# The inverse transform over w from quarters of the width, with row sums and last butterflies on GpSimd

## The chip, the cores and the metric

The kernel runs on one core of a Trainium2 chip. The metric is the device time of one execution in microseconds; a figure for a kernel is the median of several runs. The profile comes from one further execution that was recorded by the hardware profiler. Engine names are those of the profile: PE is TensorE (PEld its weight loads), DVE is VectorE, ACT is ScalarE, POOL is GpSimd, and SP is the engine whose queue issues the DMAs.

## The reference

The input x has the shape (4, 256, 256, 64), float32: batch, height h, width w, channels. Two layers follow one another. The change lies in layer 0.

```python
h  = pw(ln(x, g1, b1), w_te, b_te)                   # 64 -> 128 channels
F  = fft2(h, axes=(1, 2))
fc = gelu(pw(concat([real(F), imag(F)]), w_fc, b_fc))  # 256 -> 256
re, im = fc[..., :HID], fc[..., HID:]
sp = real(ifft2(re + 1j * im, axes=(1, 2)))
x1 = x + pw(sp, w_tp, b_tp)                          # 128 -> 64
h2 = pw(ln(x1, g2, b2), w_fe, b_fe)                  # 64 -> 128
d  = gelu(depthwise3x3(h2, w_dw) + b_dw)
x  = x1 + pw(d, w_fp, b_fp)                          # 128 -> 64
```

Layer 1 takes a moving average over h as the trend, passes the remainder through a spectral filter of 128 modes per channel, and adds both. The kernel applies it as one 256x256 matrix per channel.

## The kernel before

**Transforms.** All Fourier transforms are products with tables of cosines and sines. The forward transform over h runs in chunks of columns of x (`forward_h`): layer norm, sums and differences of mirrored columns (`halves`, L371 and L387), sums and differences of the upper and lower half of the height (`halves_h`, L394), products with the table dh (`transform`, L408), and a store to the DRAM buffer y_d. Only frequencies 0 to 128 of h are kept, since the input is real.

**Spectral stage.** The h-frequencies of an image come in groups of four (128 is carried with frequency 0), and a group is worked on in two "prs" of two frequencies each (the first group of an image has three). For one pr, `transform_w` (L502) transforms over w, `mix` multiplies by the channel matrix (ps_p, L527) with a copy to g (L539), `both` forms the product's values for +w and −w (L548), `activate` is the gelu on ACT (L552), `fold` takes a sum and a difference on GpSimd (L559), `project` multiplies by w_tp (ps_z, L584), and `turn` transposes to w-frequencies on the partitions (L597) and copies to zt (L599). When both prs of a group are in zt, `back_w` transforms back over w:

```python
for r, tbs in enumerate(((ci, nsi), (si, ci))):
    for ri, tb in enumerate(tbs):
        nc.tensor.matmul(ps[:, r * KG * C : (r + 1) * KG * C],
            tb[:, t, :], zt[:, t, ri].rearrange("p k c -> p (k c)"), ...)
```

t is the parity of the w-frequency. A group takes eight matmuls with 128 output partitions (columns 0 to 127 of w) and 256 moving columns (L618); the even part is copied (L628), and the odd part is subtracted and added (L629, L630), which gives columns 128 to 255 and 0 to 127. Two DMAs (L632) store the group in u_d.

**Convolution stage.** A chunk is eight columns of w. `load_u` (L666) loads their spectrum from u_d, `back_h` (L684) transforms back over h, `residual` (L695, L699) adds x, `measure`, `norm` and `scaled` are the layer norm (L313 to L316 on DVE, the power L322 and the scaling L327 on GpSimd), `to_channels` transposes (L722, L729), `row_sums` forms four sums and differences of neighbouring rows on DVE (L738, L742, L743), and `first`, `products`, `rest` are the matmuls of the 3x3 kernel over rows (L760, L775); gelu, projection and store follow (L826, L832, L852, L867).

**Order of work.** The order on PE, DVE, ACT and POOL is that in which the program issues (`manual_schedule`); SP's queue takes the DMAs in the order of their calls. Before the spectral stage, `starting(n)` runs 35 times (S0), with a forward chunk and two blocks of layer 1's matrices each. Then `period(n)` runs: a forward chunk at most, one group of the spectral stage (prs i and i+1, with i = 2(n − S0)), and one convolution chunk at most, each in a fixed interleaving that the call list in `period` (L1067 to L1134) writes out. Chunks of different age are in different steps: j[0] is loaded and measured, j[1] becomes row sums, j[2] and j[3] are in the products, j[4] is stored. `chunk_at` says which chunk enters in which period: the first chunk of image b may enter when the last group of that image has been stored (`opened`), at n = S0 + 35, 67, 100 and 132, and each image has 32 chunks. So there are periods of the spectral stage with the forward transform (n = 35 to 69), of all three stages (to 127), of spectral stage and convolution (to about 166), and of convolution alone, followed by layer 1.

Of the kernel before, what the change touches and what calls it, by code (L numbers as in the profile page):

```python
# [12 lines left out]
F32 = mybir.dt.float32  # L13
# [24 lines left out]
def _tables():  # L38
# [44 lines left out]
    for par in range(2):  # L83
# [6 lines left out]
    back = lambda m: np.concatenate([m[0::2, :P], m[1::2, :P]], axis=1)  # L90
# [7 lines left out]
        "ci": back(cos),  # L98
        "si": back(sin),
        "nsi": back(-sin),  # L100
# [22 lines left out]
def conv_seq_kernel(ctx: ExitStack, tc: tile.TileContext, a: dict, tables: bass.AP, out: bass.AP):  # L123
# [36 lines left out]
    ci, si, nsi = halves("ci"), halves("si"), halves("nsi")  # L160
# [171 lines left out]
    def forward_h(pool):  # L332
# [57 lines left out]
        def halves_h(j):  # L390
            xt = chunks.pop(j)
            for i, op in enumerate((ALU.add, ALU.subtract)):
                x0, x1 = (xt[:, t].rearrange("p f w c -> p (f w c)") for t in range(2))
                nc.vector.tensor_tensor(sums[j][:, i], x0, x1, op)  # L394

        def transform(j):
# [5 lines left out]
            yt = pool.tile([P, 2, 2, WH, 2, C], F32, tag="yt", name=f"yt_{j}")  # L402
# [42 lines left out]
    def spectral(pool):  # L445
# [17 lines left out]
        def begin(j):  # L463
            yb = groups[j]
            blocks = [(yb, k) for k in range(KG)]
            if j % NG == 0:

                yr = pool.tile([P, 2, 2, 2 * C], F32, tag="yr", name=f"yr_{j}", bufs=1)
                for r in range(2):
                    for part, mask in enumerate((plain, turned)):  # L470
                        at = ((r + part) % 2) * C
                        nc.vector.tensor_tensor(
                            yr[:, :, r, part * C : (part + 1) * C],
                            yb[:, :, 0, at : at + C],
                            mask.unsqueeze(2).to_broadcast([P, 2, C]),
                            ALU.mult,
                        )
                blocks = [(yr, 0), (yr, 1)] + blocks[1:]
            zt = pool.tile([P, 2, 2, KG, C], F32, tag="zt", name=f"zt_{j}")
            groups[j] = zt  # L480
            per_group[j] = [blocks[i : i + 2] for i in range(0, len(blocks), 2)]
# [109 lines left out]
        def turn(pr):  # L591

            zt, zs = groups[pr["g"]], pr["zs"]
            nf = zs.shape[1]
            ps = bank(f"ps_zt_{pr['n']}")
            for i in range(nf // P):
                nc.tensor.transpose(ps[:, i * P : (i + 1) * P], zs[:, i * P : (i + 1) * P], ident)  # L597
            nb = nf // N
            nc.scalar.copy(  # L599
                zt.rearrange("p t r k c -> p k (t r) c")[:, pr["slot"] : pr["slot"] + nb],  # L600
                ps[:, :nf].rearrange("p (j q c) -> p j q c", j=nb, c=C),
            )

        def back_w(pr):
            if not pr["last"]:
                return
            b, g = divmod(pr["g"], NG)
            if g == 0:
                u_ds[b] = spill.tile([P, N, 2, C], F32, tag="u_d", name=f"u_d_{b}")
            zt = groups.pop(pr["g"])  # L610
            ut = pool.tile([P, 2, KG, 2, C], F32, tag="ut", name=f"ut_{pr['g']}")

            pss = []
            for t in range(2):
                ps = bank(f"ps_u_{pr['g']}_{t}")
                for r, tbs in enumerate(((ci, nsi), (si, ci))):
                    for ri, tb in enumerate(tbs):
                        nc.tensor.matmul(  # L618
                            ps[:, r * KG * C : (r + 1) * KG * C],
                            tb[:, t, :],  # L620
                            zt[:, t, ri].rearrange("p k c -> p (k c)"),
                            start=ri == 0,
                            stop=ri == 1,
                        )
                pss.append(ps)
            even, odd = (ps.rearrange("p (r k c) -> p r k c", r=2, c=C) for ps in pss)
            u0, u1 = (ut[:, wt].rearrange("p k r c -> p r k c") for wt in range(2))
            nc.scalar.copy(u0, even)  # L628
            nc.vector.tensor_tensor(u1, u0, odd, ALU.subtract)  # L629
            nc.vector.tensor_tensor(u0, u0, odd, ALU.add)  # L630
            for wt in range(2):
                nc.sync.dma_start(  # L632
                    u_ds[b][g * KG : (g + 1) * KG, wt * P : (wt + 1) * P].rearrange(
                        "k p r c -> p k (r c)"
                    ),
                    ut[:, wt].rearrange("p k r c -> p k (r c)"),
                )

        def of(f):
# [13 lines left out]
            back_w=of(back_w),  # L653
        )

    def convolution(pool):
# [3 lines left out]
        TD, XN, FS = 4, 1, 2  # L660
# [4 lines left out]

        def load_u(j):  # L666
            b, q = j
            ucs[j] = pool.tile([P, W, 2, C], F32, tag="uc", name=f"uc_{name(j)}")
            nc.sync.dma_start(ucs[j], u_ds[b][:, q * W : (q + 1) * W])
# [8 lines left out]
        def back_h(j):  # L678

            uc = ucs.pop(j)  # L680
            pss = [bank(f"ps_s_{name(j)}_{i}") for i in range(2)]
            for r, tb in enumerate((ihr, ihi)):
                for i in range(2):
# [3 lines left out]
                        uc[i * C : (i + 1) * C, :, r, :],  # L687
# [45 lines left out]
        def row_sums(j):  # L733

            td = pool.tile([P, 4, NP, P], F32, tag="td", name=f"td_{name(j)}", bufs=TD)
            by_row = lambda lo: tt[:, :, lo : lo + N].rearrange("p j (i r) -> p r j i", r=2)
            for r, k in ((0, 0), (1, 3)):
                nc.vector.tensor_tensor(  # L738
                    td[:, k], by_row(0)[:, r], by_row(2)[:, r], ALU.subtract
                )  # L740
            even, odd = by_row(1)[:, 0], by_row(1)[:, 1]
            nc.vector.tensor_tensor(td[:, 1], odd, even, ALU.add)  # L742
            nc.vector.tensor_tensor(td[:, 2], odd, even, ALU.subtract)  # L743
            ts[j] = td
# [9 lines left out]
        def products(j, ks):  # L754
# [4 lines left out]
            for (k, par), ps in pss.items():  # L759
# [3 lines left out]
                    ts[j][:, k].rearrange("p j i -> p (j i)"),  # L763
# [7 lines left out]
            for k in ks:  # L771
                for g in by_turns:
# [5 lines left out]
                        td[lo : lo + C, k, at : at + n, :].rearrange("p j i -> p (j i)"),  # L778
# [100 lines left out]
        def of(f):  # L879
# [4 lines left out]
            load_x=of(load_x),  # L884
            back_h=of(back_h),
# [143 lines left out]
    def opened(b):  # L1029

        return divmod(KH * (b + 1) + 2, 2)

    chunk_at, at = {}, 0
    for b in range(B):
        at = max(at, S0 + sum(opened(b)) + 1)
# [31 lines left out]
    def period(n, f, s, c):  # L1067
# [4 lines left out]

        alone = not any(j)
        early = alone or s.done(i - 3)
# [10 lines left out]
        if alone and not s.done(i - 3):  # L1085
# [10 lines left out]
        c.row_sums(j[1])  # L1096
        s.turn(i - 2)
        s.back_w(i - 3)
        c.scaled(j[0])
        c.rest(j[3])  # L1100
        if early:
            if not alone:
                f0.square(n)
            f0.measure(n)
            f0.norm(n)
        s.mix(i)
        c.combine_rest(j[3])
        s.both(i)
        s.project(i - 1)
        s.x(i + 1)  # L1110
        if not alone or s.done(i - 3):
# [9 lines left out]
        if not early:  # L1121
            f0.square(n)
            f0.measure(n)
            f0.norm(n)
        s.turn(i - 1)
        s.back_w(i - 2)
# [9 lines left out]
    with in_order, ExitStack() as right:  # L1136
        with (
# [14 lines left out]
            for n in range(S0, S0 + opened(B - 1)[0] + 1):  # L1152
                period(n, f, s, c)
        with tc.tile_pool(name="seq", bufs=1, side="left", reuse_waits="tile") as seq:
            mts = [matrix_load(seq, c) for c in range(0, CG, CM)]
            xc = x2_load(seq, 0, 0, 1)
            for n in range(S0 + opened(B - 1)[0] + 1, END):
# [49 lines left out]
```

## Time and profile before

Three runs took 4693.13 to 4697.26 us, median 4695.19. The profiled execution took 4693.89 itself; its span is 4692.1.

| | value |
|---|---|
| median of the runs | 4695.19 us |
| profiled execution, own time | 4693.89 us |
| its span | 4692.1 us |
| granted TensorE clock | 0.99 |
| DMA | 653.31 MB, 139 GB/s on average |
| L618, return over w | 2048 records, 468.8 us |
| L738, L742, L743, row sums | 128 x 4 instructions of 128x512, 167.2 + 86.9 + 86.9 us |
| L394, halves over h | 256 of 128x512, 220.3 us |
| L559, fold on GpSimd | 520, mean 1280 ns |

How to read it: a float32 matmul leaves two records. The page gives the busy share of each engine over the whole span, and in 40 slices of about 117 us; what binds has to be read for each stage. A group of instructions is named by line, engine, operation and tiles, with its busy time, the mean of one, and the idle time of the engine ahead of it, with what ended that idle time. An arrow "<-" in brackets names the instruction whose end released it.

### The profile page before, as it was taken

What the parts mean: (1) busy time and instruction counts of PE and PEld (TensorE: products, weight loads), DVE (VectorE), ACT (ScalarE), POOL (GpSimd) and SP (SyncE); (2) the same over time, 40 slices, a digit from 0 to 9 for tenths busy, and PEclk for the clock granted to TensorE, in tenths of its full rate; (3) what the DMA queues carried; (4) which work ended last, traced back from release to release, by engine and by line L of the source; (5) the groups of instructions that cost most, each with busy time, mean ns of one, the idle gap of its engine ahead of it and who ended that gap; (6) DMA issues with size and microseconds to landing.
All of it is one profiled execution on the core that took longest, in us unless ns stands there. A gap on an engine that the chain in (4) does not pass through costs nothing.

```text
span 4692.1 us, 65967 instructions
## 1 busy us (share of the span) xinstructions
PE 4595.7 (98%) x23371; PEld 2601.2 (55%) x23371; DVE 3800.2 (81%) x6051; ACT 2511.1 (54%) x3686; POOL 1945.5 (41%) x1038
## 2 busy tenths in 40 slices
PE   8989999899999999999999999999999999999999
PEld 4545555555555555555555556556555455554444
DVE  7998888999999999999999877777777899982222
ACT  2337877666666666666666656655565333331111
POOL 4556666655555554445555334333333333320000
PEclk9999999999999999999999999999999999999999
DMA  5664444434334333333443332332332422319998
GB/s 178 199 192 144 143 133 138 126 116 125 125 125 124 125 123 125 122 121 120 124 124 119 104 100 85 107 96 90 95 96 76 157 99 98 100 59 311 324 324 277
DMA packets 759726, 653.31 MB, mean 139 GB/s; under 512 B 39693, under 2 KB 644319, under 8 KB 759272
## 3 DMA queue, kind: packets, MB, share of 16 engines
q1 hardware_dynamic: 759400, 649.11, 44.5%
q8 instruction: 187, 3.06, 0.3%
q14 instruction: 139, 1.14, 0.1%
HBM read 363.76 MB, written 285.21 MB: 138 GB/s over the span
## 4 chain that ended last, share of the span: by engine, by line
PE 87%; DVE 2%; DMA 2%; SPq 1%; ACT 0%; issue 0%; POOL 0%; DVEq 0%; POOLq 0%; ACTq 0%
PE ps_h_c L760 18%; PE ps_h_c L775 10%; PE ps_u L618 9%; PE ps_p L527 9%; PE ps_o L997 8%; PE ps_z L584 6%; PE ps_x L502 5%; PE ps_f_c L832 5%; PE ps_s_c L684 5%; PE ps_y L408 3%; PE ps_t_c L722 3%; PE ps_ft_c L852 3%; PE ps_zt L597 3%; DMA xc<-x_d 1%; DVE g L548 0%; SPq L977 0%
## 5 line engine op out<-in xcount | busy, mean ns | idle before, releaser
L559 POOL TENSOR_TENSOR g<-g 128x512 f32<-128x512 f32 (+1 forms) x520 | 660.5, 1280 | 1100.2 <-ACT g L552 996.4
L760 PE MATMUL ps_h_c<-td_c,wc_main 128*128 128x512 f32 x2048 | 921.3, 592 | 0.0
L548 DVE TENSOR_TENSOR g<-ps_p,g 128x512 f32<-128x512 f32 x1040 | 688.5, 683 | 86.6 <-ACT g L539 68.6
L552 ACT ACTIVATE g<-g,b_fc 128x1024 f32<-128x1024 f32 (+1 forms) x520 | 582.0, 1146 | 187.7 <-DVE g L548 187.6
L322 POOL TENSOR_TENSOR rstd_c<-var_c,minus_half 128x16 f32<-128x16 f32 x128 | 419.8, 3279 | 594.6 <-DVE var_c L316 594.6
L539 ACT COPY g<-ps_p 128x512 f32<-128x512 f32 (+1 forms) x520 | 302.8, 584 | 665.7 <-PE ps_p L527 660.0
L322 POOL TENSOR_TENSOR rstd<-var,minus_half 128x16 f32<-128x16 f32 x128 | 382.8, 2990 | 526.4 <-DVE var L316 403.1
L760 PEld LDWEIGHTS ps_h_c<-td_c,wc_main 128*128 128x128 f32 x2048 | 376.3, 190 | 373.7 <-issue 305.1
L775 PEld LDWEIGHTS ps_h_c<-td_c,wc_half 64*128 64x128 f32 x4032 | 416.7, 187 | 238.5 <-issue 194.1
L775 PE MATMUL ps_h_c<-td_c,wc_half 64*128 64x128 f32 (+1 forms) x4032 | 513.3, 392 | 0.0
L527 PE MATMUL ps_p<-xs,wp 64*128 64x512 f32 (+1 forms) x2080 | 498.4, 594 | 1.1 <-ACT xs L511 1.0
L618 PE MATMUL ps_u<-zt,tab 128*128 128x256 f32 x2048 | 468.8, 382 | 0.0
L997 PE MATMUL ps_o<-xc,mt 128*128 128x512 f32 x1024 | 445.0, 596 | 16.8 <-DMA xc<-x_d 16.8
L618 PEld LDWEIGHTS ps_u<-zt,tab 128*128 128x128 f32 x2048 | 383.2, 192 | 48.1 <-DVE g L548 0.3
L826 ACT ACTIVATE h_c<-h_c,b_conv 128x1024 f32<-128x1024 f32 x256 | 280.5, 1146 | 224.2 <-DVE h_c L821 224.1
L1011 DVE TENSOR_SCALAR oc<-ps_o,b_fp 128x512 f32<-128x512 f32 x128 | 96.2, 751 | 363.4 <-PE ps_o L997 342.6
L811 DVE TENSOR_TENSOR h_c<-h_c,ps_h_c 128x512 f32<-128x512 f32 x512 | 316.9, 680 | 69.7 <-PE ps_h_c L775 66.8
L800 DVE TENSOR_TENSOR h_c<-h_c,ps_h_c 128x512 f32<-128x512 f32 x256 | 175.7, 687 | 233.5 <-PE ps_h_c L775 225.0
L502 PEld LDWEIGHTS ps_x<-tab,yb 128*64 128x64 f32 x4064 | 279.1, 137 | 116.5 <-issue 88.8
L997 PEld LDWEIGHTS ps_o<-xc,mt 128*128 128x128 f32 x1024 | 195.0, 191 | 266.0 <-issue 235.3
L584 PE MATMUL ps_z<-g,w_tp 128*64 128x512 f32 x1024 | 333.7, 614 | 6.5 <-POOL g L559 3.9
L502 PE MATMUL ps_x<-tab,yb 128*64 128x128 f32 x4064 | 319.0, 274 | 0.2 <-PE ps_z L584 0.2
(125 smaller groups left out, 7205.0 us busy)
## 6 DMA issues: line engine op xcount, KB each, us to landing
y_d<-yt SPq DMA_DIRECT2D x256, 256.0 KB, 2.5
yb<-y_d SPq DMA_DIRECT2D x256, 256.0 KB, 3.1
x_c<-in_x_dram SPq DMA_DIRECT2D x128, 512.0 KB, 4.2
u_d<-ut SPq DMA_DIRECT2D x256, 256.0 KB, 2.5
uc_c<-u_d SPq DMA_DIRECT2D x128, 512.0 KB, 3.4
x_d<-st SPq DMA_DIRECT2D x128, 512.0 KB, 3.9
xc<-x_d SPq DMA_DIRECT2D x64, 1024.0 KB, 7.9
out_dram<-oc SPq DMA_DIRECT2D x256, 256.0 KB, 4.1
```

What stands on the lines that cost most here:

```text
L322: nc.gpsimd.tensor_tensor(rstd, var, minus_half.to_broadcast([P, n]), ALU.pow)
L502: nc.tensor.matmul(ps[r * C : (r + 1) * C, j * N + t * P : j * N + (t + 1) * P], blk[:, t, k, r * C : (r + 1) * C], tb[:, t, :], start=Tru ...
L527: nc.tensor.matmul(ps[:, :nf], wp[rows, cols], rhs[rows], start=True, stop=r == 1 or not pr["special"],)
L548: nc.vector.tensor_tensor(gt[:, i, :nf], re, gt[:, 1, :nf], op)
L552: nc.scalar.activation(g, g, AF.Gelu, bias=b_fc[:, half : half + 1])
L559: nc.gpsimd.tensor_tensor(g[:, 0], g[:, 0], g[:, 1], op)
L584: nc.tensor.matmul(ps[r * C : (r + 1) * C, :nf], w_tp, d[:, :nf], start=True, stop=True)
L618: nc.tensor.matmul(ps[:, r * KG * C : (r + 1) * KG * C], tb[:, t, :], zt[:, t, ri].rearrange("p k c -> p (k c)"), start=ri == 0, stop=ri == 1,
L760: nc.tensor.matmul(ps, wc_main[:, par, k, :], ts[j][:, k].rearrange("p j i -> p (j i)"), start=True, stop=False,)
L775: nc.tensor.matmul(pss[k, par][:, s * P : (s + n) * P], wc_half[lo : lo + C, k, :], td[lo : lo + C, k, at : at + n, :].rearrange("p j i -> ...
L811: nc.vector.tensor_tensor(g, g, m, (ALU.add, ALU.subtract)[r])
L997: nc.tensor.matmul(ps[:, :nf], mts[i // CM][:, i % CM, t, to * P : (to + 1) * P], xc[:, t, :, :, i, :], start=t == 0, stop=t == 1,)
```

## The change

The return over w is computed from quarters of the width. For frequencies of one parity, the tables bc (cosines) and bs (sines) cover the columns 0 to 63 only, with 64 output partitions: two groups j and j+1 are worked on together and lie in the two halves of the 128 output partitions, with real and imaginary parts side by side in 512 moving columns. A period takes four such matmuls (`back_w(n)`: parity 0 of a pair of groups in one period, parity 1 in the next). The sines are copied by ACT, and `combine_w` forms the cosine part minus and plus the sine part with real and imaginary parts swapped. `finish_w` forms the sum of both parities into `odd` and, one period later, the difference into `even` (2·even − sum), one 128x1024 instruction each on DVE, and spills each to its own buffer, u0_d and u1_d, again two DMAs in a period. Of the 256 columns, the quarters are columns 0 to 63, 65 to 128, 129 to 191 and so on, two of them in mirrored order, and `load_u` and `back_h` read those reversed, with real and imaginary parts swapped. The first columns of the other three quarters are computed apart, once for each image (`other_columns`), and column 0 gets one more addition (`first_column`); chunks at the quarters' ends are loaded in two DMAs.

Besides, `halves_h` and `row_sums` are issued on GpSimd instead of DVE. The buffers change: yt 1, zt 4 (allocated in `turn`), us 1, ut0 2, ut1 1, td in two tiles with 3 each. In `period`, the forward chunk's statistics are always taken in the middle, `back_w`, `combine_w` and `finish_w` are called once each, and `transform` is called early where there is no convolution and late where there is. Images open at n = S0 + 36, 69, 101 and 134, and the schedule is two periods longer.

```diff
-    back = lambda m: np.concatenate([m[0::2, :P], m[1::2, :P]], axis=1)
+    bc = np.zeros((P, 2, P // 2))
+    bs = np.zeros((P, 2, P // 2))
+    for par in range(2):
+        bc[:, par] = cos[par::2, : P // 2]
+        bs[:, par] = sin[par::2, : P // 2]
+        bs[:, par, 0] = 0.25 * (cos, sin)[par][par::2, P // 2]
+    bc[:, :, 0] *= 0.5
...
         def halves_h(j):
...
-                nc.vector.tensor_tensor(sums[j][:, i], x0, x1, op)
+                nc.gpsimd.tensor_tensor(sums[j][:, i], x0, x1, op)
...
+        steps, ended = {}, {}
+        for j in range(0, B * NG, 2):
+            at = (max(i for i, pr in enumerate(prs) if pr["g"] == j + 1) + 3) // 2
+            steps[at], steps[at + 1], ended[at + 2] = (j, 0), (j, 1), j
...
+        def back_w(n):
+            if n not in steps:
                 return
...
+            j, par = steps[n]
+            pss = [bank(f"ps_u_{j}_{par}_{i}") for i in range(2)]
+            for ps, tb in zip(pss, (bc, bs)):
+                for h in range(2):
+                    nc.tensor.matmul(
+                        ps[h * C : (h + 1) * C],
+                        tb[:, par, :],
+                        groups[j + h][:, par].rearrange("p r k c -> p (r k c)"),
+                        start=True,
+                        stop=True,
+                    )
+            if par:
+                del groups[j], groups[j + 1]
+            us = pool.tile([P, 2, KG, C], F32, tag="us", name=f"us_{j}_{par}", bufs=1)
+            nc.scalar.copy(us.rearrange("p r k c -> p (r k c)"), pss[1])
+            parts[n] = pss[0].rearrange("p (r k c) -> p r k c", r=2, c=C), us
...
+        def combine_w(n):
...
+            nc.vector.tensor_tensor(dst[:, 0], cs, us[:, ::-1], ALU.subtract)
+            nc.vector.tensor_tensor(dst[:, 1], cs[:, ::-1], us, ALU.add)
+            half_sums.setdefault(j, []).append(ut)
...
+        def finish_w(n):
+
+            flat = lambda t: t.rearrange("p k q r c -> p (k q r c)")
+            if n in ended:
+                j = ended[n]
+                even, sums = half_sums.pop(j)
+                nc.vector.scalar_tensor_tensor(
+                    flat(even), flat(even), 2.0, flat(sums), ALU.mult, ALU.subtract
+                )
+                spill_w(j, 1, even)
+            if n in steps and steps[n][1]:
...
+                nc.vector.tensor_tensor(flat(odd), flat(even), flat(odd), ALU.add)
+                spill_w(j, 0, odd)
...
+            for h in range(2):
+                k = (g + h) * KG
                 nc.sync.dma_start(
+                    u_ds[b][i][k : k + KG].rearrange("k q s r c -> s (k q) (r c)"),
+                    ut[h * C : (h + 1) * C].rearrange("p k q r c -> p (k q) (r c)"),
                 )
...
+        quarters = ((0, 0, False), (1, 1, True), (1, 0, False), (0, 1, True))
...
+        def first_column(j):
+            if j[1] == 0:
+                col = ucs[j][:, 0]
+                nc.vector.tensor_tensor(col, col, firsts.pop(j)[:, ::-1], ALU.add)
...
+        def other_columns(j):
...
+            for i in range(2):
+                nc.sync.dma_start(v[:, 2 * i : 2 * i + 2], u_ds[b][i][:, :, 0])
...
+            nc.sync.dma_start(fixed[b], v[:, 3:6])
...
-                        uc[i * C : (i + 1) * C, :, r, :],
+                        uc[i * C : (i + 1) * C, ::-1, 1 - r, :]
+                        if down
+                        else uc[i * C : (i + 1) * C, :, r, :],
...
         def row_sums(j):
...
+            nc.gpsimd.tensor_tensor(ts[j][1], odd, even, ALU.add)
+            nc.gpsimd.tensor_tensor(ts[j][2], odd, even, ALU.subtract)
             for r, k in ((0, 0), (1, 3)):
-                nc.vector.tensor_tensor(
-                    td[:, k], by_row(0)[:, r], by_row(2)[:, r], ALU.subtract
+                nc.gpsimd.tensor_tensor(
+                    ts[j][k], by_row(0)[:, r], by_row(2)[:, r], ALU.subtract
                 )
-            even, odd = by_row(1)[:, 0], by_row(1)[:, 1]
-            nc.vector.tensor_tensor(td[:, 1], odd, even, ALU.add)
-            nc.vector.tensor_tensor(td[:, 2], odd, even, ALU.subtract)
...
         c.scaled(j[0])
         c.rest(j[3])
-        if early:
-            if not alone:
-                f0.square(n)
-            f0.measure(n)
-            f0.norm(n)
+        c.row_sums(j[1])
+        if not alone:
+            f0.square(n)
+        f0.measure(n)
+        f0.norm(n)
         s.mix(i)
         c.combine_rest(j[3])
+        s.back_w(n - S0)
         s.both(i)
+        s.combine_w(n - S0)
         s.project(i - 1)
         s.x(i + 1)
-        if not alone or s.done(i - 3):
+        if not alone:
             f2.transform(n - 2)
         fn.load(n + 1)
         c.activate(j[3])
...
+        c.other_columns(j[0])
         s.turn(i - 1)
-        s.back_w(i - 2)
+        s.finish_w(n - S0)
         s.activate(i, 0)
         s.activate(i, 1)
         s.fold(i)
```

## The prediction

> **What bounds the kernel now.** I read the busy totals and slices of the page first, then its chain and its costliest groups, then the stretches of each stage, and last the timeline of one period of each stage.
>
> ```profile
> PE 4595.7 (98%) x23371; PEld 2601.2 (55%) x23371; DVE 3800.2 (81%) x6051; ACT 2511.1 (54%) x3686; POOL 1945.5 (41%) x1038
> ...
> PE   8989999899999999999999999999999999999999
> ...
> DVE  7998888999999999999999877777777899982222
> ...
> POOL 4556666655555554445555334333333333320000
> ...
> L559 POOL TENSOR_TENSOR g<-g 128x512 f32<-128x512 f32 (+1 forms) x520 | 660.5, 1280 | 1100.2 <-ACT g L552 996.4
> L618 PE MATMUL ps_u<-zt,tab 128*128 128x256 f32 x2048 | 468.8, 382 | 0.0
> ```
> TensorE is at 98%, and the return over w (L618) is 469 us of it. VectorE stands at 90% and more in the middle; GpSimd looks free at 41%. That last figure is an average, so I go by stage (stretch, length, busy time of PE, PEld, DVE, ACT, POOL, clock, DMA share, GB/s):
>
> ```profile
> 60.00:330.00 270.00, 264.73 (x929) 156.49 (x927) 266.96 (x354) 97.17 (x145) 154.40 (x60) 1.00 0.63 197
> 390.00:850.00 460.00, 460.00 (x2638) 266.08 (x2637) 396.06 (x605) 366.47 (x542) 293.73 (x181) 1.00 0.47 138
> 960.00:2590.00 1630.00, 1626.47 (x9199) 952.76 (x9196) 1533.91 (x2482) 1011.60 (x1484) 819.92 (x438) 1.00 0.40 123
> 2640.00:3640.00 1000.00, 999.25 (x5704) 594.59 (x5702) 761.43 (x1258) 585.02 (x863) 365.79 (x215) 1.00 0.30 93
> 3690.00:4180.00 490.00, 490.00 (x2383) 266.40 (x2382) 450.19 (x747) 189.70 (x268) 155.25 (x60) 1.00 0.28 94
> ```
> Starting (matrices beside the forward transform) is VectorE's: 267 of 270. The other four are TensorE's: the spectral stage alone (about 35 periods of 15.34 us), all three stages (57 of 29.65), spectral with convolution (37), convolution only (33 of 16.4). In the second stretch GpSimd is busy 64%, the most of the four, and there its work stands in a loop:
>
> ```profile
> 516.00 2.54 POOL L559 TENSOR_TENSOR g<-g 128x512 f32<-128x512 f32 x2 [3.21 <-PE ps_u L618]
> 519.08 0.59 PE L584 MATMUL ps_z<-g,w_tp 128*64 128x512 f32 x1
> 520.38 1.88 PE L408 MATMUL ps_y<-xb,tab 128*64 128x512 f32 x7
> 522.78 1.99 PE L527 MATMUL ps_p<-xs,wp 64*128 64x512 f32 x8
> 524.93 2.74 DVE L548 TENSOR_TENSOR g<-ps_p,g 128x512 f32<-128x512 f32 x4 [1.60 <-ACT g L539]
> 527.58 1.28 DVE L371 TENSOR_TENSOR xb<-xt 128x512 f32<-128x512 f32 x2
> 527.71 3.62 PE L618 MATMUL ps_u<-zt,tab 128*128 128x256 f32 x16
> 528.90 1.29 DVE L387 TENSOR_TENSOR xt<-xb 128x512 f32<-128x512 f32 x2
> 530.23 1.29 DVE L394 TENSOR_TENSOR xb<-xt 128x512 f32<-128x512 f32 x2
> ```
> Columns: start, duration, engine, line, operation, out<-in, count. A fold ends at 518.54; its projection, the next product ps_p and the products of L548 follow, done by 527.58, 9.04 us later. The last lines (halves over w, halves over h) hang on that end only by VectorE's order; nobody on GpSimd waits for them.
>
> **What the Trainium skill says.** TensorEngine Tiling (Array Packing), Theoretical Speedup: an output side of at most 64 allows up to twice the rate. The trace agrees: four 64-wide matmuls of 512 columns (L408; a matmul leaves two records) take 1.81 us start to start in a period of all three stages, eight 128-wide ones of 256 columns (L618), as many columns in all, 3.46. GPSIMD Engine Reference, 3.1: a GpSimd tensor_tensor add is priced 1.96 times VectorE's; here 1280 ns (L559) against 693 (L738), 1.85 times. The same page, section 7, puts a higher price on reads that step over 8 bytes; the new row sums step exactly 8, and no row shows that. SBUF — State Buffer, Who interferes with whom: a VectorE instruction with two SBUF inputs and a GpSimd instruction that reads SBUF exclude each other. The trace agrees, and both sides pay:
>
> ```profile
> 905.87 3.11 POOL L559 TENSOR_TENSOR g<-g 128x512 f32<-128x512 f32 x2
> 907.89 3.95 DVE L387 TENSOR_TENSOR xt<-xb 128x512 f32<-128x512 f32 x2
> 916.20 1.08 PE L597 MATMUL ps_zt<-ident,zs 128*128 128x128 f32 x4 [4.20 <-ACT zs L588]
> 917.07 4.92 PE L618 MATMUL ps_u<-zt,tab 128*128 128x256 f32 x16
> ```
> Undisturbed those pairs take 2.54 and 1.29. The last two lines are what an idle of 4.20 us does to TensorE: 1.08 for 0.66 and 4.92 for 3.62, together 1.7 us more.
>
> **The change, part by part.**
>
> *Return over w on TensorE.* Per period eight 128x256-column matmuls become four of 64-wide form: 3.46 goes, 1.81 comes, −1.65 us. Over 130 periods that is 214 us if TensorE is what ends the period.
>
> *VectorE per period of all three stages.* Row sums leave: 2×0.69 + 2×0.68 = 2.74 (in the trace with GpSimd's waits near 2.4 net). Halves over h leave: 2×0.65, 1.3. The two combines replace L629 and L630 one for one. One finishing operation on 128x1024 with two SBUF inputs comes: 1.21 by the row of L695. From 28.4 to about 25.9.
>
> *GpSimd per period of all three.* From 15.2 us: 4×1.28 of row sums and 2×1.28 of halves, 7.7, to 22.9. Their collisions with VectorE's two-input operations cost each side about 2 us.
>
> *Starting, 35 periods of 9.16.* VectorE-bound; L394 there takes 2.82 for two behind GpSimd, and leaves. But GpSimd must now deliver before L408, and TensorE has 264.73 of 270. I take −8; 0 to −20.
>
> *Spectral alone, the step that decides.* GpSimd's order in a period becomes: power, halves over h of the chunk before (2), fold of one group (2), scaling, fold of the other (2). The fold now queues behind halves over h, which wait for the halves over w on VectorE, which queue behind the combine, which queues behind the products of L548. And those hang on the previous period's fold, by the chain read above. So a loop closes: fold end to products' end 9.04; combine 1.41; halves over w 2.61; halves over h 2×1.28 = 2.56; fold 2.54; handoffs 0.1: 18.26 us, against 15.34 now. Nothing in it overlaps. Onto it: the finishing operation stands on VectorE directly behind the halves over w and waits for nothing, so it takes the shared read first: +1.15, 19.4. TensorE's own work in the period is about 13.5, so it idles over 4 us in one piece, ahead of the projection that the loop goes through; by the two lines above that is a slower clock, +1.7 (bounds 0 and, if all TensorE pieces of the loop run cold, 2.9): 21.1. Over 34 periods: (21.1 − 15.34)×34 = +195. Bounds: the bare loop +100, with the lock +138, everything cold +235.
>
> *All three, 57 periods.* TensorE 29.65 − 1.65 = 28.0; VectorE 25.9 and about 2 of port waits, 28. GpSimd's queue (power 3.3, scaling 2.0, row sums 5.1, power 2.95, halves, fold) now ends shortly before the fold's projection is due. So not all of 1.65 is realised: −1.2 each, −68; bounds −20 and −94.
>
> *Spectral with convolution, 37 periods.* VectorE is at 76%, GpSimd at 37%, no halves there: −1.65 each, −61.
>
> *Convolution only, 33 periods.* Row sums queue on GpSimd behind power and scaling of the next chunk. In the trace scaling ends at 3967.26, row sums end 5.12 later at 3972.4, and the row products of 16.37 later have little left: +0.45 each, +15; bounds 0 and +60.
>
> *Seams, four images.* A new chunk's columns now come from a finished pair: finishing operation at the period's end, spill 2.5, load 3.4 by the page's DMA table, and the return over h stands first on TensorE in the next period: 5 to 6 us each where there was half a period or more of slack. On top come nine small operations and the small loads and a store of the other three columns on SP's queue, and two periods more in the schedule (168 to 170). +25; bounds 10 and 50.
>
> *Layer 1.* Untouched: 0. The split loads at quarter ends stay under a period of slack: 0.
>
> Sum: −8 + 195 − 68 − 61 + 15 + 25 = +98. The profiled execution took 4693.89 itself (span 4692.1), so 4791.9; the median of the runs shown, 4695.19, is 1.3 above that execution, well inside every bound. I take **4792**.
>
> **Rivals.**
> - *The fold does not close a loop* (faster). If the engines' slack lets halves over h run early enough, spectral alone stays at 15.34 or falls by 1.65: 4597 down to 4541, about 4570. For it: TensorE holds the chain at 87% and only that was cut. Against it: GpSimd's order, where the fold cannot pass halves over h.
> - *Row sums are dear on GpSimd.* At 8-byte steps 1.9 us each instead of 1.28, +2.5 a period: all three loses 0.5 where it should gain 1.2 (+97), convolution only +13: 4902. For it: no GpSimd row with such a step. Against: the skill's threshold lies above 8 bytes.
> - *The bare loop.* Lock and clock cost nothing: spectral alone +100, sum +3, about 4697. For it: GpSimd may get its read first, and the idle may split in two. Against: the lines at 905 and 916.
>
> **How the numbers follow.** The forecast (4720 to 4880) gets 0.62, no loop 0.14, dear row sums 0.14, the bare loop 0.10. The range 4690 to 4900 holds the first, half of the third and half of the fourth, near 0.8. A difference below 0.2% (9 us) cannot be told from none. Faster: no loop 0.14 and a fifth of the bare loop, 0.16; same 0.04; slower 0.80.
>
> **What would show it.** Spectral alone near 21 us a period, TensorE idle about 6 of them in front of ps_z with GpSimd's fold as releaser, and slower matmuls after; all three near 28.4; spectral with convolution shorter by 1.6; row sums near 1.28 each. It is wrong if the period of spectral alone is below 17, if the folds do not wait for halves over h, or if a seam costs more than 15 us.

## The result, and the profile after

The changed kernel took 4723.49 us in the median of four runs (4718.87 to 4729.3), the kernel before 4694.16 beside it (4691.67 to 4697.26): a ratio of 1.0063 with a 95% interval of 1.0045 to 1.008. That is 29 us slower, where the prediction had 97 and a range of 4690 to 4900. The sign was right, and so was the mechanism in the stage that decides it, the spectral stage alone; the size was more than three times too large, above all through the term for all three stages. The profiled execution took 4729.3 us itself, with a span of 4727.5.

The page of the changed kernel, the lines that answer to those shown of before:

```profile
PE 4438.6 (94%) x22347; PEld 2295.4 (49%) x22347; DVE 3607.9 (76%) x5451; ACT 2529.2 (53%) x3686; POOL 2796.4 (59%) x1806
...
PE   8987777778999999999999999999999899999999
...
DVE  7886667678999999999999877777778688871222
...
POOL 5876666668887878688878655555555455530000
PEclk9998888889999999999999999999999999999999
...
L565 POOL TENSOR_TENSOR g<-g 128x512 f32<-128x512 f32 (+1 forms) x520 | 703.9, 1364 | 632.0 <-ACT g L558 632.0
```

The fourth to ninth slices are new: TensorE is at 70 to 79% there, its clock at 0.8. The stretches say the same (stretch, length, PE, PEld, DVE, ACT, POOL, clock, DMA share, GB/s):

```profile
390.00:850.00 460.00, 342.55 (x1792) 165.47 (x1792) 313.37 (x425) 278.57 (x405) 292.30 (x182) 0.83 0.37 101
2130.00:2330.00 200.00, 200.00 (x1153) 105.08 (x1149) 190.72 (x290) 134.88 (x197) 159.34 (x101) 1.00 0.45 135
2900.00:3400.00 500.00, 500.00 (x2917) 269.90 (x2915) 387.25 (x619) 314.91 (x462) 264.76 (x192) 1.00 0.35 102
```

In the first of them, the spectral stage alone, no engine is full, which is what a loop of waits between engines looks like. In the other two TensorE is full as it was before.

The starts of the groups ps_y, ps_u and ps_o in the two traces give the time by stage:

| from, to | before | after | difference | forecast |
|---|---|---|---|---|
| start to the 33rd ps_y (starting) | 340.5 | 334.8 | −5.7 | −8 |
| to the 68th ps_y (spectral alone) | 533.3 | 696.5 | +163.2 | +195 |
| to the last ps_y (all three) | 1763.7 | 1653.5 | −110.2 | −68 |
| to the last ps_u (spectral, convolution) | 995.5 | 968.3 | −27.2 | −61 |
| to the first ps_o (convolution only) | 593.0 | 598.4 | +5.4 | +15 |
| layer 1 | 466.1 | 476.1 | +10.0 | 0 |
| seams, lying in the rows above | | | | +25 |
| sum | 4692.1 | 4727.5 | +35.4 | +98 |

Layer 1's 10 us are no part of the change: with the same code, the profiled executions of this study have 464 to 478 us there, and one kernel that was profiled twice had 476 and 473. Steady periods went from 15.34 to 20.48 us (spectral alone), from 29.47 and later 29.81 to 27.73 (all three), from 27.75 to 26.01 (spectral with convolution), and stayed at 16.37 (convolution only).

One thing shifts between two rows: images open later now, so two chunks of the convolution move from the row of all three stages to the next one. By the starts of ps_s_c the two rows hold 60 and 36 chunks before, 58 and 38 after. A chunk is worth some 14 us there (an estimate: 29.47 − 15.34).

The timeline of one period of the spectral stage alone, changed kernel (start, duration, engine, line, operation, count, and in brackets the idle time before and its releaser):

```profile
513.95 2.50 POOL L565 TENSOR_TENSOR g<-g 128x512 f32<-128x512 f32 x2
515.27 2.34 PE L590 MATMUL ps_z<-g,w_tp 128*64 128x512 f32 x3 [5.13 <-POOL g L565]
...
519.97 1.89 PE L416 MATMUL ps_y<-xb,tab 128*64 128x512 f32 x7
...
522.38 1.99 PE L533 MATMUL ps_p<-xs,wp 64*128 64x512 f32 x8
...
524.52 2.74 DVE L554 TENSOR_TENSOR g<-ps_p,g 128x512 f32<-128x512 f32 x4 [6.19 <-ACT g L545]
...
527.18 0.68 DVE L652 TENSOR_TENSOR ut<-ps_u,us 128x512 f32<-128x512 f32 x1
...
528.37 1.28 DVE L379 TENSOR_TENSOR xb<-xt 128x512 f32<-128x512 f32 x2
...
529.69 1.29 DVE L395 TENSOR_TENSOR xt<-xb 128x512 f32<-128x512 f32 x2
530.90 1.22 DVE L671 SCALAR_TENSOR_TENSOR ut<-ut,ut 128x1024 f32<-128x1024 f32 x1
531.15 3.33 POOL L402 TENSOR_TENSOR xb<-xt 128x512 f32<-128x512 f32 x2 [3.42 <-DVE xt L395]
...
534.45 2.48 POOL L565 TENSOR_TENSOR g<-g 128x512 f32<-128x512 f32 x2
535.76 2.34 PE L590 MATMUL ps_z<-g,w_tp 128*64 128x512 f32 x3 [5.13 <-POOL g L565]
```

This is the predicted loop, link by link: fold, ps_z, ps_p, the products of L554, combine (L652), halves over w, halves over h on GpSimd (3.33 for two, with the finishing operation L671 just ahead of it on VectorE), the next fold. TensorE idles 5.13 us ahead of ps_z, and the three ps_z then take 2.34.

### The profile page after: what moved, and what is told of

Read it like the earlier page. It is cut to its first block, busy times and chain, and to the rows that moved or that the text cites. A ratio compares the mean times of both kernels' runs of the same rounds, so it can differ in the third digit from the quotient of the medians.

```text
span 4727.5 us, 63507 instructions
## 1 busy us (share of the span) xinstructions
PE 4438.6 (94%) x22347; PEld 2295.4 (49%) x22347; DVE 3607.9 (76%) x5451; ACT 2529.2 (53%) x3686; POOL 2796.4 (59%) x1806
## 4 chain that ended last, share of the span: by engine, by line
PE 81%; DVE 6%; POOL 5%; issue 4%; DMA 2%; ACT 2%; SPq 1%; POOLq 0%; DVEq 0%; ACTq 0%
PE ps_h_c L865 18%; PE ps_h_c L880 10%; PE ps_o L1104 8%; PE ps_p L533 7%; PE ps_z L590 5%; PE ps_x L508 5%; PE ps_f_c L937 5%; PE ps_y L416 5%; PE ps_s_c L784 4%; PE ps_u L629 4%; PE ps_t_c L824 3%; PE ps_ft_c L957 3%; POOL xb L402 2%; PE ps_zt L607 2%; DVE g L554 1%
## 5 line engine op out<-in xcount | busy, mean ns | idle before, releaser
L565 POOL TENSOR_TENSOR g<-g 128x512 f32<-128x512 f32 (+1 forms) x520 | 703.9, 1364 | 632.0 <-ACT g L558 632.0
L554 DVE TENSOR_TENSOR g<-ps_p,g 128x512 f32<-128x512 f32 x1040 | 687.5, 682 | 233.3 <-ACT g L545 215.3
L330 POOL TENSOR_TENSOR rstd_c<-var_c,minus_half 128x16 f32<-128x16 f32 x128 | 371.8, 2905 | 478.5 <-DVE var_c L324 468.8
L590 PE MATMUL ps_z<-g,w_tp 128*64 128x512 f32 x1024 | 354.2, 670 | 195.9 <-POOL g L565 192.5
L402 POOL TENSOR_TENSOR xb<-xt 128x512 f32<-128x512 f32 x256 | 350.9, 1390 | 220.5 <-DVE xt L395 215.1
L1104 PE MATMUL ps_o<-xc,mt 128*128 128x512 f32 x1024 | 450.9, 603 | 20.3 <-DMA xc<-x_d 20.3
L330 POOL TENSOR_TENSOR rstd<-var,minus_half 128x16 f32<-128x16 f32 x128 | 372.8, 2913 | 64.1 <-DMA xt<-in_x_dram 34.6
L508 PEld LDWEIGHTS ps_x<-tab,yb 128*64 128x64 f32 x4064 | 297.3, 149 | 149.4 <-issue 129.4
L508 PE MATMUL ps_x<-tab,yb 128*64 128x128 f32 x4064 | 345.3, 295 | 0.0
L1116 ACT ACTIVATE oc<-ps_o,b_fp 128x512 f32<-128x512 f32 x128 | 87.9, 687 | 384.5 <-PE ps_o L1104 307.5
```

The lines of the kernel that those rows point to most:

```text
L330: nc.gpsimd.tensor_tensor(rstd, var, minus_half.to_broadcast([P, n]), ALU.pow)
L402: nc.gpsimd.tensor_tensor(sums[j][:, i], x0, x1, op)
L508: nc.tensor.matmul(ps[r * C : (r + 1) * C, j * N + t * P : j * N + (t + 1) * P], blk[:, t, k, r * C : (r + 1) * C], tb[:, t, :], start=Tru ...
L554: nc.vector.tensor_tensor(gt[:, i, :nf], re, gt[:, 1, :nf], op)
L565: nc.gpsimd.tensor_tensor(g[:, 0], g[:, 0], g[:, 1], op)
L590: nc.tensor.matmul(ps[r * C : (r + 1) * C, :nf], w_tp, d[:, :nf], start=True, stop=True)
```

## The experiments

All start from the changed kernel. Times are medians, or a single run where no interval stands. The period is that of the spectral stage alone unless said otherwise, as a mean over 24 steady periods, taken from the starts of ps_y. In some runs single periods alternate between two or more lengths; where the recorded expectations name such a period (19.45 for the first run), it is the median.

### Halves over h: which engine, and where in the order

First, back on VectorE:

```diff
-                nc.gpsimd.tensor_tensor(sums[j][:, i], x0, x1, op)
+                nc.vector.tensor_tensor(sums[j][:, i], x0, x1, op)
```

> The changed kernel with one part undone: halves over h are issued on VectorE again. Loop theory (the fold queues behind halves over h on GpSimd, which hang on the previous fold): the loop opens, a period of the spectral stage alone falls from 20.5 us to about 14.4 (TensorE 13.7, VectorE with 1.3 more near 14.4), the whole to about 4723 - 33 x 6 + 10 = 4535 us. Rival A (GpSimd is simply too slow for its 12 us of work with the collisions): the period falls by what leaves GpSimd, 2.6 to 3.4, to about 17.5, the whole to about 4625. Rival B (TensorE's low clock holds the period up by itself): the period stays over 19.

Measured: 4690.09 us, 0.9996 of before (0.9987 to 1.0005). The period is 19.3 (single ones 18.2 to 20.4), not 14.4. Of the three expectations only the last gives the right number, and for another reason: TensorE's clock is 0.97 in the stage, and most of the stage's chain lies on VectorE. The timeline:

```profile
714.53 1.28 DVE L379 TENSOR_TENSOR xb<-xt 128x512 f32<-128x512 f32 x2
...
715.85 2.36 DVE L395 TENSOR_TENSOR xt<-xb 128x512 f32<-128x512 f32 x2
716.21 3.13 POOL L565 TENSOR_TENSOR g<-g 128x512 f32<-128x512 f32 x2 [2.31 <-ACT g L558]
...
718.25 3.95 DVE L402 TENSOR_TENSOR xb<-xt 128x512 f32<-128x512 f32 x2
719.31 2.34 POOL L335 TENSOR_TENSOR xt<-xt,rstd 128x1024 f32<-128x1024 f32 x1
```

Each pair on VectorE takes 1.29 when it is alone. Here halves over w run into the fold and halves over h into fold and scaling, 2.36 and 3.95: 3.7 us of waiting, and the finishing operation (in one period of this trace 2.92 us for 1.21) still stands ahead of the next products. The same stretch of the kernel before:

```profile
528.90 1.29 DVE L387 TENSOR_TENSOR xt<-xb 128x512 f32<-128x512 f32 x2
529.63 0.59 ACT L628 COPY ut<-ps_u 128x512 f32<-128x512 f32 x1 [1.14 <-PE ps_u L618]
530.12 2.19 ACT L552 ACTIVATE g<-g,b_fc 128x1024 f32<-128x1024 f32 x2
530.23 1.29 DVE L394 TENSOR_TENSOR xb<-xt 128x512 f32<-128x512 f32 x2
531.35 2.55 POOL L559 TENSOR_TENSOR g<-g 128x512 f32<-128x512 f32 x2 [3.20 <-PE ps_u L618]
```

There the gelu (L552) stood on ACT behind the copy of ps_u, so the fold began 3.77 us after the products' end at 527.58, when VectorE's two-input operations were all but done. The new return over w comes earlier, and the combine stands ahead of the halves: the fold and the halves now meet. That this order is why they meet is read from the two timelines; no run puts the old order back by itself. The period is long with halves over h on either engine; only the chain differs.

Second, on GpSimd, but behind the fold:

```diff
-        f1.halves_h(n - 1)
+        if not alone:
+            f1.halves_h(n - 1)
...
         s.fold(i)
+        if alone:
+            f1.halves_h(n - 1)
```

> Halves over h stay on GpSimd, but in the spectral stage alone they are issued behind the fold that they preceded. GpSimd has the same work in another order. Loop theory: the fold no longer waits for VectorE's halves over w, the period falls from 20.5 to about 13.8 (TensorE's own work), the whole to about 4723 - 33 x 6.7 = 4502 us. Rival A (too much work on GpSimd): the period stays at 20.5, the whole near 4720. Rival B (clock): over 19.

Measured: 4609.77 us, 0.9818 (0.9803 to 0.9832), most periods 16.91, the mean 17.0. GpSimd has the same work, so the order is shown to be worth about 3.5 us a period, and rivals A and B fall. Part of the 3.5 comes with the shorter idle of TensorE: its clock is 0.99 in this run's stage, where the changed kernel has 0.83. But 13.8 was not reached. The chain of this run goes over the fold (4.01 us for two, beside the finishing operation's 2.29), halves over h, and ps_y, which now waits for them.

### The finishing operation and the clock, each by itself

```diff
+        if alone:
+            s.finish_w(n - 1 - S0)
         s.mix(i)
...
-        s.finish_w(n - S0)
+        if any(chunk_at.get(n + 1 - k) for k in range(5)):
+            s.finish_w(n - S0)
```

> In the spectral stage alone the finishing operation on VectorE (128x1024, two SBUF inputs) moves from right behind the halves over w to the middle of the next period, where VectorE idles 6 us. The loop itself stays. Port theory (it takes the shared read just before halves over h, which then take 3.33 us for two instead of 2.55): the period falls by 0.8 to 1.2 us, from 20.5 to about 19.5, the whole by about 30 us. Without that price: no change.

Measured: 4702.85 us, period 19.76 (single ones 19.2 to 20.3), which is 0.7 less. Halves over h return from 3.33 to 2.50 for two. The price is real and a little over half of the 1.15 in the forecast.

```diff
         s.mix(i + 1)
+        if alone:
+            ps = bank(f"warm_{n}")
+            for _ in range(4):
+                nc.tensor.matmul(ps, ident, tab[:, :512], start=True, stop=True)
```

> In each period of the spectral stage alone four matmuls of 128x512 are added, written to a bank that nobody reads, where TensorE idles 5.1 us before ps_z. Clock theory (the idle costs about 1.1 us of slower matmuls in the loop): the matmuls after the wait return to 1.1 us for three ps_z and 0.6 for nine ps_x, the period falls from 20.5 to about 19.4 although TensorE has 3.4 us more to do, the granted clock in the stage rises from 0.83 to 1.00. If the clock costs nothing in the loop: 20.5 stays. The output is the same.

Measured: 4661.23 us, period 18.79, clock 1.00 in the stage. The timeline from the added matmuls on:

```profile
539.26 3.70 PE L1238 MATMUL warm<-tab,ident 128*128 128x512 f32 x8
...
544.47 1.86 PE L590 MATMUL ps_z<-g,w_tp 128*64 128x512 f32 x3 [1.50 <-POOL g L565]
...
546.60 0.71 PE L508 MATMUL ps_x<-tab,yb 128*64 128x128 f32 x9
```

3.70 us of work that nobody needs make every period 1.69 shorter. The three ps_z take 1.86 rather than 2.34, and part of that is now a wait for the fold's second half; nine ps_x take 0.71, where the run without these matmuls needed 2.07 for eleven. The gain is more than the 1.1 expected here. It equals the 1.7 of the prediction, but that figure was read from other matmuls (ps_zt and ps_u, behind an idle of 4.20 us), so that it fits this closely is partly luck.

### The change without its moves to GpSimd

Halves over h and row sums back on VectorE (nc.gpsimd replaced by nc.vector in `halves_h` and `row_sums`).

> The changed kernel with both moves to GpSimd undone: row sums and halves over h on VectorE, the new return over w and its new order stay. Row-sum theory (VectorE is next in the stage of all three, and moving the row sums is what lets TensorE's gain show): VectorE has 26.5 + 1.3 + 2.7 us, above TensorE's 27.7, so a period of all three rises from the 27.83 of the run with halves over h on VectorE to 29.5 to 30, the whole from 4690 to about 4790 us. Rival (TensorE stays the bound there in any case): 27.8 and about 4690. In the spectral stage alone both expect 19.4, as in that run, since there are no row sums in it. The power in the convolution should take 3.28 us again if it is the row sums on VectorE that lengthen it, 2.90 if not.

Measured: 4925.79 us, 1.0498 (1.0481 to 1.0516). The period of the spectral stage alone is 19.4, as expected. Those of all three alternate between 30.5 and 34.4, 32.4 in the mean, well over the 29.5 to 30 expected; the rival, 27.8, falls. A stretch of a little over four periods:

```profile
1406.00:1543.30 137.30, 123.97 (x678) 65.08 (x677) 132.64 (x195) 80.14 (x118) 67.67 (x35) 0.98 0.38 114
```

VectorE is busy 97%, TensorE 90%. Against the run with only halves over h on VectorE (27.83), the row sums' move is worth 4.6 us a period, more than the 2.7 us of their own length. How much of that is VectorE's load and how much its fixed order with the statistics in mid-period was not separated. The mean of the power (L330, convolution) in this run, and in the run with the row sums on GpSimd, from the groups of each:

```profile
L330 POOL TENSOR_TENSOR rstd_c<-var_c,minus_half 128x16 f32<-128x16 f32 x128 | 421.1, 3290 | 614.3 <-DVE var_c L324 573.2 <-PE ps_h_c L880 41.2
```

```profile
L330 POOL TENSOR_TENSOR rstd_c<-var_c,minus_half 128x16 f32<-128x16 f32 x128 | 371.8, 2905 | 480.8 <-DVE var_c L324 444.1 <-PE ps_h_c L880 36.7
```

The row sums on VectorE are what lengthened the power to 3.29. Undone in this sequence, the change's parts are worth: the new return over w in its new order about +235 us (by the same rows as in the table +119 in the spectral stage alone and +139 in all three), the row sums' move on top of it −236, the move of halves over h on top of both +33. In another sequence the shares could differ.

### Towards a faster version

Late halves over h and the finishing operation elsewhere, the two diffs above together:

> Halves over h on GpSimd behind the fold, and the finishing operation moved to the middle of the next period, both in the spectral stage alone. In the run with halves over h behind the fold the period was 16.91 us, with the fold at 4.01 us for two because it shares the read with the finishing operation. Port theory: the fold returns to 2.5, the period falls by 1.3 to 1.5 to about 15.5, the whole to about 4560 us. If the collision only moves elsewhere: 16.9 stays.

Measured: 4587.19 us, period 15.94, between the 15.5 and the 16.9 of the two expectations. The fold takes 3.04 for two rather than 4.01, since it still meets the end of the halves over w.

To that, the transform over h late in the period, as in the other stages (`f2.transform(n - 2)` called behind `s.x(i + 1)` only):

> As the one before, and in the spectral stage alone the transform over h is issued late in the period, as it is in the other stages, so that TensorE does not wait for halves over h that now stand behind the fold. Loop theory (the last wait of TensorE in this stage is for halves over h): the period falls to 13.6 to 14.2, TensorE's own work, the whole to about 4510. Port theory (what binds next is the shared read itself, folds 5.1, scaling 1.9, halves over h 2.55, halves over w 2.58, finishing 1.22, in all 13.35 us of a period, and handoffs): 14.5 to 15.5, the whole about 4540.

Measured: 4603.10 us, a miss for both: periods alternate between 17.1 and shorter ones down to 15.4, 16.6 in the mean. TensorE no longer waits for halves over h, but VectorE is late instead: in this trace even the small operations of the statistics meet GpSimd's reads (L322 takes 1.90 us for 0.2, L324 1.30 for 0.2), the power takes 3.82, and in one of two periods read the halves over w take 3.32 for 1.29.

Halves over h on VectorE in every stage, in the spectral stage alone behind the next products, and the finishing operation in mid-period (in part):

```diff
         s.both(i - 1)
+        if alone and n > S0:
+            f2.halves_h(n - 2)
```

> Halves over h on VectorE, but in the spectral stage alone issued behind the next products of L554 and not ahead of them, and the finishing operation in the middle of the next period. The shared read then has 12.1 us in a period. Theory from the run with halves over h on VectorE (19.45: halves, halves over h and the finishing operation stood in VectorE's chain ahead of the products and collided with fold and scaling): the chain opens, 14 to 15 us a period, the whole about 4540 us. If VectorE's total is what binds: over 17.

Measured: 4640.95 us, period 17.55: the number of the second expectation, though the chain of this run changes between VectorE and TensorE. Halves over h take 3.02 for 1.29 there, and ps_y waits for them.

As the fastest (the late halves over h with the finishing operation elsewhere), but ps_y behind ps_p on TensorE (`f2.transform(n - 2)` behind `s.mix(i)`):

> As the run with late halves and the finishing operation elsewhere (15.94 us a period of the spectral stage alone), but there the transform over h stands on TensorE behind the products ps_p and not ahead of them, with its copies on ACT behind those of g. Theory from its chain (fold, halves over h, ps_y, then ps_zt and ps_p that only stand behind ps_y in TensorE's order): the loop opens, the period falls to 13.7 to 14.5, the whole to about 4587 - 33 x 1.7 = 4530 us. Rival (the shared read, 13.35 us of each period, with handoffs and collisions): 15 to 16, about 4570.

Measured: 4595.21 us, a miss for both: periods alternate between 17.3 and shorter ones down to 15.2, 16.6 in the mean. TensorE's wait for halves over h is gone, and the chain in the 22 us that were read is VectorE's from end to end, with 3.32 and 2.37 for pairs of 1.29.

As the fastest, but images open one period earlier (`at = max(at, S0 + opened(b) + 1)`, `c.other_columns(j[1])`):

> As the run with late halves and the finishing operation elsewhere, but an image's convolution opens one period earlier, and the first columns of the other quarters are computed in its second period. Seam theory (the later opening and the wait for the finished pair cost about 10 us an image, 40 in all): 20 to 40 us less, 4550 to 4567. If the first chunk then waits on TensorE's queue for the spill and load of the last pair, as it stands first in its period: no gain, 4580 to 4590, with an idle of 5 us or more before ps_s_c at each image.

Measured: 4616.83 us, 30 more. For the tile uc_c in this run, what its engine sat idle for (us in total, times):

```profile
  DVE uc_c L742: 36.2, 4
  DMA first<-u_d: 28.7, 3
```

Four times some 9 us: TensorE waits for the addition to column 0, which waits for the load of a column that was just stored. This is the wait of the second expectation, larger than expected there. The later opening costs less than the wait that it avoids.

Halves over h on VectorE at their old place in the spectral stage alone, on GpSimd elsewhere, finishing operation in mid-period (in part):

```diff
-        f1.halves_h(n - 1)
+        f1.halves_h(n - 1, nc.vector if alone else nc.gpsimd)
```

> In the spectral stage alone halves over h are issued on VectorE at their old place, directly behind the halves over w, and the finishing operation in the middle of the next period; elsewhere as in the changed kernel, on GpSimd. The shared read has 12.1 us in a period instead of 13.35 and VectorE's chain ahead of the next products is that of the kernel before. Theory (the collisions of the finishing operation and the 1.28 us pieces on GpSimd are what held the stage over 15.9): 14.0 to 15.0 us a period, the whole 4540 to 4560 us. If collisions of fold and scaling with the halves remain, as in the first run with halves over h on VectorE (19.45): 16 to 18, the whole 4590 to 4650.

Measured: 4642.10 us, 0.9889 (0.9876 to 0.9903), period 18.0, as the second expectation has it. The collisions are those of the first run:

```profile
708.42 2.37 DVE L395 TENSOR_TENSOR xt<-xb 128x512 f32<-128x512 f32 x2
708.70 3.22 POOL L565 TENSOR_TENSOR g<-g 128x512 f32<-128x512 f32 x2 [1.47 <-ACT g L558]
...
710.83 3.95 DVE L402 TENSOR_TENSOR xb<-xt 128x512 f32<-128x512 f32 x2
```

So the place of the finishing operation costs 1.4 of the 19.3. The halves still meet fold and scaling; what the period would be without that, this run does not show. Last, the fastest again:

> The fastest kernel so far, with halves over h behind the fold and the finishing operation in the middle of the next period, timed in rounds: 15.94 us a period of the spectral stage alone and 27.73 of all three as in its first look, 4580 to 4595 us, faster than before by 2.1 to 2.4%.

Measured: 4582.48 us, 0.9761 (0.9747 to 0.9774), period 15.95. It beats both kernels, the one before by 2.4%. In six orders the mean period of this stage did not get under 15.9 (single periods reached 15.2), though TensorE's own work would allow some 13.6 (an estimate: 15.34 less the 1.74 that left it). At their undisturbed lengths VectorE's operations with two SBUF inputs and GpSimd's folds, scaling and halves over h take 13.35 us of each such period together (12.1 with halves over h on VectorE), and where they meet they lengthen each other, as the lines above show. That these meetings are the floor is a guess: it is compatible with the six runs, but none of them tests it by itself.

## Why the prediction was wrong, and where it was right

The step that failed is the term for all three stages, and within it the discount for VectorE and for GpSimd's queue. It is taken first.

- **All three stages: −68 forecast, −110 measured in its row.** "So not all of 1.65 is realised: −1.2 each, −68" rested on VectorE at 28 us a period and on a GpSimd queue that ends shortly before the fold's projection is due. No wait followed from either. VectorE is busy 190.72 us in 200, 26.4 a period, TensorE 200 of 200. In one period of the trace:

```profile
1411.65 2.52 POOL L402 TENSOR_TENSOR xb<-xt 128x512 f32<-128x512 f32 x2 [1.15 <-DVE xt L395]
1414.12 3.50 POOL L565 TENSOR_TENSOR g<-g 128x512 f32<-128x512 f32 x2
...
1418.96 1.08 PE L590 MATMUL ps_z<-g,w_tp 128*64 128x512 f32 x4
```

  GpSimd is early enough to wait 1.15 us for VectorE's halves over w, and its fold, although lengthened to 3.50, ends at 1417.62, 1.34 ahead of the projection. GpSimd was also faster than priced: row sums 1.05 and not 1.28 each, the power 2.90 and not 3.28, since its collision partner went away with the row sums. But these 1.3 us would mostly have gone into that wait (an estimate from the lines), so the discount would have been wrong at the forecast's prices too. TensorE kept all that left it, −1.74 in the first half: over 57 periods this is 31 us more than the forecast. Some 10 us more come from the second half, where the difference is −2.08, because the kernel before waited there for its fold. Four lines of its timeline show it, the fold and its projection in the first and in the second half:

```profile
1400.61 2.51 POOL L559 TENSOR_TENSOR g<-g 128x512 f32<-128x512 f32 x2 [6.48 <-ACT g L552]
1406.47 1.08 PE L584 MATMUL ps_z<-g,w_tp 128*64 128x512 f32 x4
```

```profile
2025.16 2.51 POOL L559 TENSOR_TENSOR g<-g 128x512 f32<-128x512 f32 x2
2027.37 1.43 PE L584 MATMUL ps_z<-g,w_tp 128*64 128x512 f32 x4
```

  In the first half the fold is done 3.3 us before the projection starts; in the second it ends at 2027.67, inside the projection.
- **The loop of the spectral stage alone: right.** Its links stand in the trace as forecast. The terms: the bare loop 18.26, and measured 18.1 if the two prices are taken off (20.48 − 0.7 − 1.69). The clock 1.7, measured 1.69. The shared read 1.15, measured 0.7. Together 21.1, measured 20.48.
- **Its number of periods: mis-sized.** It was multiplied by 34; the first four periods, while the stage fills, lost only 5.7 us together. The other 31 lost 5.08 each. +195 became +163.
- **Spectral with convolution and the seams.** The steady period fell by 1.74, forecast 1.65; over 37 periods that is −64, where the row has −27. About 28 us of the gap (an estimate) are the two chunks that came over from the row above. That row lost this work, yet its total is no more than what its steady periods account for, so something there took about as much. Both rows together stand some 36 us above their steady differences. I put them down to the later openings, forecast at 25 for all four; no run isolates them.
- **Convolution only: right that row sums are nearly hidden.** The period stayed at 16.37; +0.45 a period did not come.
- **Starting: right** (−5.7 for −8).
- **The rivals.** Dear row sums: refuted, at 1.05 us each. The bare loop: refuted by the runs on the clock and on the finishing operation, which both have a price. No loop: refuted by the timeline and by the run with halves over h behind the fold. The chance given to the range does not follow from its parts: they add up to 0.74, not to near 0.8.

Against the forecast's +98, the trace has +35: −32 from the spectral stage alone, −42 from all three stages, −10 from convolution only, and +21 from the rest (the row of spectral with convolution against the seams' 25, starting, layer 1).

One expectation drawn from the right loop failed with it: that halves over h on GpSimd were the cause, so that VectorE would cure it. The run with only the new return over w has 19.4 us in the spectral stage alone. The move of halves over h closed one loop, and beneath it lay a chain on VectorE of nearly the same length.

## What to carry to other kernels

A move between VectorE and GpSimd is to be priced by the order on both and by what meets what, not by busy shares: here the same two instructions behind the fold instead of ahead of it were worth about 3.5 us a period, and with one more operation moved the whole went from 0.6% slower than the kernel before to 2.4% faster. A discount for an engine that ends shortly before it is needed should name the wait that it stands for; here there was none. Before a loop is blamed on one link, look for what closes next when that link is opened. And an idle engine that sits in a loop can be worth filling: a stretch in which TensorE waited 5 us ran faster with 3.7 us of useless matmuls in the wait.

## What had not been expected of the hardware

- GpSimd's row sums (128x512, both inputs stepping 8 bytes) take 1046 to 1059 ns, the fold of the same size, with inputs and output in one tile, 1280 undisturbed. No run here says why.
- GpSimd's power, which reads only 128x16 elements, takes 2905 ns, and 3290 in the run with the row sums on VectorE.
- Collisions come in rows: in the first run the meeting of halves over w and fold is followed by those of halves over h with the fold and with the scaling, 3.7 us in a period for two pairs that are 1.29 long each.
